# RWKV on one Trainium2 core: repeating a unit's values by DMA instead of by matmul, with the recurrence in place

## The chip, the core and the metric

The kernel runs on one core of one Trainium2 chip. A core has a matrix engine (PE, with a separate row in the profile, PEld, for its weight loads), a vector engine (DVE), an activation engine (ACT), a general engine (POOL) and a sequencer that only issues transfers (SP). Transfers that SP and ACT issue are carried by the same 16 DMA engines. The engines run on their own and meet at semaphores. The engines that compute read and write the on-chip memory SBUF, 128 partitions wide; matmuls write PSUM, which has 8 banks of 128 x 512 floats. DRAM is reached by DMA alone.

The metric is the time of one execution on the device in microseconds (us). All data is float32.

## What is computed

Four layers are applied in turn to x of shape 16 x 100 x 512 (batch, steps, channels): a cross attention, an RWKV block, a second cross attention with a feed-forward part, and a second RWKV block. The change touches the two RWKV blocks, which are alike. Of one block this part matters (h = 32 heads of s = 16 channels):

```python
r = (xr @ Wr.T).reshape(b, l, h, s_)
k = (xk @ Wk.T).reshape(b, l, h, s_)
v = (xv @ Wv.T).reshape(b, l, h, s_)
g = jax.nn.silu(xg @ Wg.T)
...
def step(s, rkvw):
    r_t, k_t, v_t, w_t = rkvw
    a = k_t[..., :, None] * v_t[..., None, :]
    out = jnp.einsum('bhi,bhij->bhj', r_t, u * a + s)
    s = a + w_t[..., :, None] * s
    return (s, out)
```

Each head so has a state of 16 x 16 numbers (i of k, j of v) for each of the 16 batch rows, and 100 steps that follow one another. Around it lie a layer norm, mixes of neighbouring steps, the projections with their 512 x 512 weights, a norm over each head, the output projection, and a channel block of three more 512 x 512 projections.

## The kernel before

The 16 batch rows are worked on in NG = 4 groups of G = 4, so that a row of T = 400 numbers holds 4 batch rows of L = 100 steps. The 512 channels are NC = 4 pieces of 128. A pair of group and piece is a chunk, C = 0 to 15. A chunk has 128 channels x 16 values of j, which are 16 rows of states for each channel; they are done in 8 units of 128 partitions x 2 rows x 400. There are 128 units a block, u = 0 to 127; `where(u)` (line 1129) gives a unit's chunk C, its j group jg (four of the sixteen j) and rp (which two of the four 32-channel rows, r, it takes). On a unit's 128 partitions lie 4 values of j times 32 channels (2 heads of 16).

A unit needs k, w and r of its channels, the same for all four jq of its partitions, and v of its four j, the same for all 16 i of a head.

- `projections` (line 799) computes k, w, v, r and the gate g of a group, and `store` (line 806) sends each 128 x 400 piece from ACT's queue into a DRAM tile `put[g]` laid out [chunk, r, 32 channels, T]. There are 20 such stores a group; those of group 0 come before the first unit, those of groups 1 to 3 beside the units of the group before.
- `enter(C)` (line 1089), four units before a chunk begins, loads v, k and r back as 128 x 400 pieces (`vc`, `kc`, `rc`) for the bonus term `u * a`, and `repeat(C, 0)`; `repeat(C, 1)` follows two units later. `repeat` (line 1099) fills `kr`, `wr` and `rr`, 128 x 2 x 400 each and three buffers each, by four transfers of 32 partitions for each operand: one for each jq. `gates` (line 1203) loads g back.
- `spread(u + 1)` (line 1132) repeats v on 16 partitions: two calls of `mm` (four matmuls in the trace) with a 0/1 matrix `sel` (line 691) put v of the four j into the two rows of a PSUM tile `vb`, shifted by one step; ACT then copies the initial state of each batch row into the first step.
- `product(u)` (line 1147): DVE multiplies `vb` by `kr` in PSUM. `scan(u)` (line 1156): two DVE scans, one a row, run the recurrence over `wr` and `vb` into an SBUF tile `a`; POOL multiplies `a` by `rr`.
- `gather` (line 1166), every second unit, sums over i by four calls of `mm` (eight matmuls in the trace) into the PSUM bank `acc`, and after a chunk `norm` makes the head norm and the gating on ACT, POOL and PE.

The loop at line 1231 writes the order of the work out by hand: `u` runs from -42 past 128, and between the parts of a unit `pieces`, a list of projections and channel-block work with costs in us, is taken until the budget `due` of the step is used up (2.5, 2.95 or 3.9 us). PE, DVE, ACT and POOL issue in that order, since `mm`, `vector`, `scalar` and `gpsimd` (lines 79 to 82) pin it. SP's instructions are not pinned: a scheduler puts its transfers where it finds them ready. PSUM holds two `vb` of two banks each, `acc`, and three banks `mm` for all else. When the time comes, `load(n, "Wfk", "Wfr", "Wfv")` (line 1248) fetches the three channel-block weights, 1 MB each, into a ring of five weight tiles.

Of the kernel before, what the change touches and what calls it, by code (L numbers as in the profile page):

```python
# [17 lines left out]
G = 4  # L18
# [17 lines left out]
def xattn_sequence(ctx: ExitStack, tc: tile.TileContext, d: dict, out: bass.AP):  # L36
# [42 lines left out]
    vector, scalar, gpsimd = InOrder(nc.vector), InOrder(nc.scalar), InOrder(nc.gpsimd)  # L79
# [556 lines left out]
    def rwkv(n, ws, next_weights, last):  # L636
# [6 lines left out]
        with ExitStack() as es:  # L643
# [6 lines left out]
            vbs = [psum.tile([128, 2, 512], F32, name=f"vb{i}") for i in range(2)]  # L650
            acc = psum.tile([128, 512], F32, name="acc")
            slots = Slots([psum.tile([128, 512], F32, name=f"mm{i}") for i in range(3)])
# [35 lines left out]

            fold = one.tile([128, 32], F32, name="fold")
            nc.vector.tensor_reduce(fold, ident.rearrange("p (r s) -> p s r", s=32), AX.X, ALU.add)  # L690
            sel = one.tile([128, 16, 32], F32, name="sel")
            for j in range(16):
                nc.vector.tensor_copy(
                    sel[:, j, :].rearrange("p (h i) -> p h i", i=16),
                    fold.rearrange("p (h j) -> p h j", j=16)[:, :, j : j + 1].to_broadcast([128, 2, 16]),
                )
# [101 lines left out]

            def projections(g, base):
                nm = f"{n}_{g}"  # L800
                to = put[g] = {
                    t: dram.tile([NC, 4, 32, T], F32, tag=t, name=f"d{t}_{nm}")
                    for t in ("k", "v", "r", "w", "g")
                }

                def store(t, c, tile):
                    nc.scalar.dma_start(out=to[t][c].rearrange("r p t -> (r p) t"), in_=tile)
# [163 lines left out]
            def channels(g, slot):  # L971
# [41 lines left out]
                def keys(co):  # L1013
                    def read(ps):
                        if co == 0:
                            st["kk"] = two.tile([128, NC, T], F32, tag="kk", bufs=1, name=f"kk_{nm}")
# [19 lines left out]
                def values(i):  # L1036
                    b = g * G + i

                    def read(ps):
                        def add():  # L1040
# [3 lines left out]
                            if last:  # L1044
                                nc.sync.dma_start(out=out[b], in_=xb[b])
# [43 lines left out]
            def enter(C):  # L1089
# [4 lines left out]
                for k, bufs in (("v", 2), ("k", 1), ("r", 1)):  # L1094
                    t[k] = two.tile([128, T], F32, tag=f"{k}c", bufs=bufs, name=f"{k}c_{n}_{C}")
                    nc.sync.dma_start(out=t[k], in_=put[g][k][c].rearrange("r p t -> (r p) t"))
                repeat(C, 0)

            def repeat(C, rp):
                g, c = C // NC, C % NC  # L1100
                rep = chunks[C]["rep"][rp] = {}
                for t in ("k", "w", "r"):
                    rep[t] = two.tile([128, 2, T], F32, tag=f"{t}rep", bufs=3, name=f"{t}r_{n}_{C}_{rp}")
                    for jq in range(4):
                        nc.sync.dma_start(
                            out=rep[t][32 * jq : 32 * jq + 32],
# [124 lines left out]
            while u < UNITS + 6 or pieces or slots.due:  # L1231
# [15 lines left out]
                if u == UNITS - 32 - 3:  # L1247
                    cm.update(load(n, "Wfk", "Wfr", "Wfv"))
# [448 lines left out]
```

## Time and profile before

| what | value |
| --- | --- |
| median of 3 runs | 3563.27 us (3559.06 to 3570.37) |
| the profiled execution: its own time | 3563.91 us |
| its span in the profile | 3561.8 us |
| busy in the span: PE, PEld | 3252.8 (91%), 1434.5 (40%) |
| busy in the span: DVE, ACT, POOL | 1768.5 (50%), 972.8 (27%), 1374.2 (39%) |
| transfers issued by SP, share of the 16 engines | 177.59 MB, 17.3% |
| transfers issued by ACT, share of the 16 engines | 32.78 MB, 2.6% |
| PE's matmuls vb<-vc,sel: count, busy | 1024, 260.8 us |
| recurrence of block 1: first product, last multiply by r starts | 859.5 us, 1506.4 us |
| recurrence of block 3: first product, last multiply by r starts | 2819.4 us, 3465.6 us |

Busy time is the sum of the time in which an engine had an instruction of the program at work; idle time in front of a group says what ended it. An arrow `a<-b,c` names the tile written and those read, with buffer numbers left out. PE's matmuls are pipelined, so that a busy PE is not a PE at its peak. The time of the execution is 2.1 us more than its span. A window of the profile is a stretch of time from the span's start; it gives the busy time of each engine inside it, the granted PE clock (1.0 is full), the busy share of the 16 DMA engines, and the rate in GB/s.

### The profile page before, as it was taken

How to read it: one execution, taken by the hardware profiler on the slowest of the kernel's cores; microseconds unless marked ns; L12 is line 12 of the kernel's file. 1: busy time of each engine (PE TensorE's matmuls, PEld its weight loads, DVE VectorE, ACT ScalarE, POOL GpSimd, SP SyncE). 2: the span in 40 equal slices, each digit the busy share in tenths (PEclk: the TensorE clock that was granted, in tenths of full speed). 3: DMA queues.
4: the chain of work that ended last, by engine and by line, in shares of the span. 5: the costliest groups of instructions: out<-in, count | busy, mean ns of one | idle time of the engine just before them, and what ended most of it. 6: DMA issues, size and time to landing. Idle time of an engine off the chain costs nothing. (4 is left out here: it accounts for less than half of the span.)

```text
span 3561.8 us, 45408 instructions
## 1 busy us (share of the span) xinstructions
PE 3252.8 (91%) x17411; PEld 1434.5 (40%) x17411; DVE 1768.5 (50%) x3570; ACT 972.8 (27%) x1699; POOL 1374.2 (39%) x1036
## 2 busy tenths in 40 slices
PE   6999998868999988989999999699998899998898
PEld 3444443334333333334455455344443433333333
DVE  4777777723767755523333333400001386775551
ACT  1323222322333333322222322201111233333332
POOL 1444444543666655412212112200002366665541
PEclk8999999978999989989999999899998899998998
DMA  5010101022434342011000010200011243434300
GB/s 167 21 30 21 30 21 33 1 65 82 134 101 136 116 130 77 14 52 35 19 19 19 27 31 21 74 0 0 0 47 49 83 138 101 136 116 119 86 27 16
DMA packets 151074, 213.26 MB, mean 60 GB/s; under 512 B 22942, under 2 KB 131294, under 8 KB 150858
## 3 DMA queue, kind: packets, MB, share of 16 engines
q1 hardware_dynamic: 127818, 177.59, 17.3%
q10 hardware_dynamic: 23040, 32.78, 2.6%
q8 instruction: 137, 2.24, 0.3%
q14 instruction: 79, 0.65, 0.1%
HBM read 174.25 MB, written 36.04 MB: 59 GB/s over the span
## 5 line engine op out<-in xcount | busy, mean ns | idle before, releaser
L77 POOL TENSOR_TENSOR a<-a,rr 128x800 f32<-128x800 f32 x256 | 480.5, 1878 | 342.1 <-DVE a L77 265.4
L77 DVE TENSOR_TENSOR_SCAN a<-wr,vb 128x400 f32<-128x400 f32 x512 | 475.7, 970 | 19.3 <-PE acc L82 9.7
L77 DVE TENSOR_TENSOR vb<-vb,kr 128x792 f32<-128x792 f32 x256 | 250.5, 979 | 197.1 <-ACT vb L77 195.5
L77 DVE CUSTOM_DVE_ANT_0 junk<-l_sc,mask 100x361 f32<-100x361 f32 x512 | 273.0, 533 | 89.9 <-PE l_sc L82 73.4
L82 PE MATMUL vb<-vc,sel 32*128 32x396 f32 x1024 | 260.8, 566 | 2.4 <-ACT th L77 1.3
L77 DVE TENSOR_TENSOR pt<-l_sc,maskT 121x400 f32<-121x400 f32 x384 | 193.5, 566 | 91.9 <-PE l_sc L82 91.0
L77 ACT ACTIVATE pt<-pt 121x1600 f32<-121x1600 f32 x96 | 147.6, 1538 | 284.2 <-DVE pt L77 282.6
L1425 DVE CUSTOM_DVE_ANT_0 junk<-l2a_sc,mask 100x361 f32<-100x361 f32 x256 | 136.9, 535 | 173.0 <-PE l2a_sc L82 155.8
L63 PE MATMUL p<-l_proj,h 128*100 128x512 f32 x512 | 220.4, 593 | 0.0
L77 POOL TENSOR_TENSOR xj<-tm,ext 128x400 f32<-128x400 f32 x160 | 152.5, 960 | 170.3 <-DVE tm L77 165.2
L77 DVE SCALAR_TENSOR_TENSOR tm<-mm,vec,sx 128x400 f32<-128x400 f32 x160 | 99.8, 631 | 229.3 <-PE mm L82 184.3
L1617 DVE TENSOR_TENSOR x<-p,x 100x512 f32<-100x512 f32 x16 | 11.1, 691 | 379.3 <-PE p L63 340.2
L1461 POOL TENSOR_TENSOR pa<-pt,pt 121x1600 f32<-121x1600 f32 x16 | 57.2, 3573 | 366.7 <-ACT pt L1456 366.7
L63 PE MATMUL h<-yTb,l_fc 128*128 128x400 f32 x512 | 175.4, 505 | 7.9 <-ACT yTb L229 7.9
L82 PE MATMUL v<-l_v_w,ct 128*121 128x512 f32 x384 | 179.9, 614 | 0.0
L82 PE MATMUL k<-ct,l_k_w 128*128 128x361 f32 x512 | 172.8, 481 | 7.7 <-DVE mv_l2a L207 7.7
L77 POOL TENSOR_TENSOR pa<-pt,pt 121x1600 f32<-121x1600 f32 x32 | 114.7, 3583 | 167.0 <-ACT pt L77 167.0
L82 PE MATMUL l_sc<-kz,qz 32*100 32x361 f32 x1024 | 116.0, 523 | 42.6 <-DVE pt L77 21.6
L77 ACT COPY vb<-s0r 128x8 f32<-128x8 f32 x256 | 43.1, 168 | 408.7 <-PE vb L82 318.6
L82 PEld LDWEIGHTS vb<-vc,sel 32*128 32x128 f32 x1024 | 85.3, 190 | 145.5 <-issue 105.3
L63 PEld LDWEIGHTS p<-l_proj,h 128*100 128x100 f32 x512 | 85.7, 167 | 133.2 <-issue 132.6
L63 PEld LDWEIGHTS h<-yTb,l_fc 128*128 128x128 f32 x512 | 98.4, 193 | 82.9 <-ACT yTb L229 9.8
(254 smaller groups left out, 5317.3 us busy)
## 6 DMA issues: line engine op xcount, KB each, us to landing
kr<-dk SPq DMA_DIRECT2D x256, 100.0 KB
wr<-dw SPq DMA_DIRECT2D x256, 100.0 KB
rr<-dr SPq DMA_DIRECT2D x256, 100.0 KB
ct<-in_ctxT SPq DMA_DIRECT2D x32, 722.0 KB
dk<-k ACTq DMA_DIRECT2D x32, 200.0 KB
kc<-dk SPq DMA_DIRECT2D x32, 200.0 KB
dw<-wd ACTq DMA_DIRECT2D x32, 200.0 KB
dv<-v ACTq DMA_DIRECT2D x32, 200.0 KB
```

Of the source, the lines that this page charges most:

```text
L63: nc.tensor.matmul(out=ps, lhsT=lhs(c), rhs=rhs(c), start=(c == 0), stop=(c == n - 1))
L77: return lambda *args, **kw: tc.keep_in_program_order(op(*args, **kw))
L82: pin(nc.tensor.matmul(**kw))
L1425: nc.vector.tensor_tensor_reduce(out=junk, in0=ss[r][:L, :S2], in1=t["mask"], scale=-1.0, scalar=FLT_MAX, op0=ALU.add, op1=ALU.min, accum_ ...
L1461: nc.gpsimd.tensor_tensor(t["pa"], t["pt"][0], pt, ALU.add)
L1617: nc.vector.tensor_tensor(x, ps[:L, :], x, ALU.add)
```

## The change

- `sel`, `vb` and `spread` are gone. `fetch(u + 2)` loads a unit's v straight into its tile `a` by one transfer from DRAM, whose source names each row of 2 x 400 numbers 16 times; `first(u + 1)` lets ACT write the initial states into `a`. `product` multiplies `a` by `kr` in place, and the two scans run in place in `a`, which has six buffers instead of four. Source and destination of all of this are in SBUF.
- `repeat` uses one transfer for each operand, whose source repeats its 32 rows 4 times from the outside; the operands are now asked for one by one, at steps 4 to 7 of the chunk before, and r of the second half at step 0 of its own chunk. For this k, w, r and g lie in DRAM as [chunk, 32 channels, r, T], and v as one row of numbers, [chunk, j, h, r, T], one number late, so that a row read at its start gives the step before. `rows_of` makes the matching patterns: v's stores and loads become four transfers of 32 partitions each.
- SP's transfers of the RWKV blocks are pinned to source order. The channel-block weights are fetched in four parts each, one a step, from three fixed steps on.
- The five PSUM banks of `vb` and the three `mm` become seven `mm`, and `kk` moves into the ring of `xm`.

```diff
--- before.py
+++ after.py
@@ -76,7 +76,7 @@
...
-    vector, scalar, gpsimd = InOrder(nc.vector), InOrder(nc.scalar), InOrder(nc.gpsimd)
+    vector, scalar, gpsimd, sync = map(InOrder, (nc.vector, nc.scalar, nc.gpsimd, nc.sync))
@@ -647,9 +647,8 @@
...
-            vbs = [psum.tile([128, 2, 512], F32, name=f"vb{i}") for i in range(2)]
             acc = psum.tile([128, 512], F32, name="acc")
-            slots = Slots([psum.tile([128, 512], F32, name=f"mm{i}") for i in range(3)])
+            slots = Slots([psum.tile([128, 512], F32, name=f"mm{i}") for i in range(7)])
@@ -686,15 +685,6 @@
...
-            fold = one.tile([128, 32], F32, name="fold")
-            nc.vector.tensor_reduce(fold, ident.rearrange("p (r s) -> p s r", s=32), AX.X, ALU.add)
-            sel = one.tile([128, 16, 32], F32, name="sel")
-            for j in range(16):
-                nc.vector.tensor_copy(
-                    sel[:, j, :].rearrange("p (h i) -> p h i", i=16),
-                    fold.rearrange("p (h j) -> p h j", j=16)[:, :, j : j + 1].to_broadcast([128, 2, 16]),
-                )
@@ -796,15 +786,28 @@
...
+            def rows_of(g, t, c):
+
+
+                if t == "v":
+                    n0 = 1 + c * 128 * T
+                    rows = put[g]["v"][n0 : n0 + 128 * T].rearrange("(j h r t) -> r h j t", h=2, r=4, t=T)
+                    return [(slice(32 * r, 32 * r + 32), rows[r]) for r in range(4)]
+                return [(slice(0, 128), put[g][t][c].rearrange("p r t -> r p t"))]
+
             def projections(g, base):
                 nm = f"{n}_{g}"
                 to = put[g] = {
-                    t: dram.tile([NC, 4, 32, T], F32, tag=t, name=f"d{t}_{nm}")
-                    for t in ("k", "v", "r", "w", "g")
+                    t: dram.tile([NC, 32, 4, T], F32, tag=t, name=f"d{t}_{nm}")
+                    for t in ("k", "r", "w", "g")
                 }
 
+                to["v"] = dram.tile([NC * 128 * T + 1], F32, tag="v", name=f"dv_{nm}")
+                sync.dma_start(out=to["v"][0:1].rearrange("(p t) -> p t", t=1), in_=eps[0:1, :])
+
                 def store(t, c, tile):
-                    nc.scalar.dma_start(out=to[t][c].rearrange("r p t -> (r p) t"), in_=tile)
+                    for ps, rows in rows_of(g, t, c):
+                        nc.scalar.dma_start(out=rows, in_=tile[ps])
@@ -1013,7 +1016,7 @@
...
-                            st["kk"] = two.tile([128, NC, T], F32, tag="kk", bufs=1, name=f"kk_{nm}")
+                            st["kk"] = two.tile([128, NC, T], F32, tag="xm", bufs=3, name=f"kk_{nm}")
@@ -1042,7 +1045,7 @@
...
-                                nc.sync.dma_start(out=out[b], in_=xb[b])
+                                sync.dma_start(out=out[b], in_=xb[b])
@@ -1093,19 +1096,19 @@
                 t = chunks[C] = {"rep": {}}
                 for k, bufs in (("v", 2), ("k", 1), ("r", 1)):
                     t[k] = two.tile([128, T], F32, tag=f"{k}c", bufs=bufs, name=f"{k}c_{n}_{C}")
-                    nc.sync.dma_start(out=t[k], in_=put[g][k][c].rearrange("r p t -> (r p) t"))
-                repeat(C, 0)
-
-            def repeat(C, rp):
+                    for ps, rows in rows_of(g, k, c):
+                        sync.dma_start(out=t[k][ps], in_=rows)
+                repeat(C, 0, "k")
+
+            def repeat(C, rp, names):
                 g, c = C // NC, C % NC
-                rep = chunks[C]["rep"][rp] = {}
-                for t in ("k", "w", "r"):
+                rep = chunks[C]["rep"].setdefault(rp, {})
+                for t in names:
                     rep[t] = two.tile([128, 2, T], F32, tag=f"{t}rep", bufs=3, name=f"{t}r_{n}_{C}_{rp}")
-                    for jq in range(4):
-                        nc.sync.dma_start(
-                            out=rep[t][32 * jq : 32 * jq + 32],
-                            in_=put[g][t][c, 2 * rp : 2 * rp + 2].rearrange("r p t -> p r t"),
-                        )
+                    k = put[g][t][c, :, 2 * rp : 2 * rp + 2, :]
+                    sync.dma_start(
+                        out=rep[t], in_=bass.AP(k.tensor, k.offset, [[0, 4], [4 * T, 32], [1, 2 * T]])
+                    )
 
             def bonus(C, part):
 
@@ -1129,24 +1132,27 @@
             def where(u):
                 return u // 8, u % 8 // 2, u % 2
 
-            def spread(u):
+            def fetch(u):
 
                 C, jg, rp = where(u)
-                p4 = vbs[u % 2][:, :, :T].rearrange("p r (b t) -> p r b t", t=L)
-                for i in range(2):
-                    rs = slice(64 * rp + 32 * i, 64 * rp + 32 * i + 32)
-                    mm(
-                        out=p4[:, i, :, 1:L], lhsT=sel[rs, 4 * jg : 4 * jg + 4, :].rearrange("p q m -> p (q m)"),
-                        rhs=steps(chunks[C]["v"][rs, :])[:, :, 0 : L - 1], start=True, stop=True,
-                    )
+                g, c = C // NC, C % NC
+                a = products[u] = two.tile([128, 2, T], F32, tag="a", bufs=6, name=f"a_{n}_{u}")
+                v = put[g]["v"]
+                n0 = v.offset + ((c * 16 + 4 * jg) * 8 + 2 * rp) * T
+                sync.dma_start(out=a, in_=bass.AP(v.tensor, n0, [[4 * T, 8], [0, 16], [1, 2 * T]]))
+
+            def first(u):
+
+                C, jg, rp = where(u)
                 g = C // NC
                 scalar.copy(
-                    p4[:, :, :, 0], s0r[:, 2 * rp : 2 * rp + 2, C % NC, jg, g * G : (g + 1) * G]
+                    products[u].rearrange("p r (b t) -> p r b t", t=L)[:, :, :, 0],
+                    s0r[:, 2 * rp : 2 * rp + 2, C % NC, jg, g * G : (g + 1) * G],
                 )
...
             def product(u):
                 C, jg, rp = where(u)
-                p4 = vbs[u % 2][:, :, :T].rearrange("p r (b t) -> p r b t", t=L)
+                p4 = products[u].rearrange("p r (b t) -> p r b t", t=L)
@@ -1156,11 +1162,9 @@
             def scan(u):
                 C, jg, rp = where(u)
                 rep = chunks[C]["rep"][rp]
-                a = products[u] = two.tile([128, 2, T], F32, tag="a", bufs=4, name=f"a_{n}_{u}")
+                a = products[u]
                 for i in range(2):
-                    vector.tensor_tensor_scan(
-                        a[:, i, :], rep["w"][:, i, :], vbs[u % 2][:, i, :T], 0.0, ALU.mult, ALU.add
-                    )
+                    vector.tensor_tensor_scan(a[:, i, :], rep["w"][:, i, :], a[:, i, :], 0.0, ALU.mult, ALU.add)
                 gpsimd.tensor_tensor(a, a, rep["r"], ALU.mult)
@@ -1205,7 +1209,7 @@
...
-                nc.sync.dma_start(out=chunks[C]["g"], in_=put[g]["g"][c].rearrange("r p t -> (r p) t"))
+                sync.dma_start(out=chunks[C]["g"], in_=rows_of(g, "g", c)[0][1])
@@ -1244,13 +1248,16 @@
...
-                if u == UNITS - 32 - 3:
-                    cm.update(load(n, "Wfk", "Wfr", "Wfv"))
+                for k, at_u in (("Wfk", UNITS - 46), ("Wfr", UNITS - 40), ("Wfv", UNITS - 35)):
+                    if 0 <= u - at_u < NC:
+                        load_part(cm, n, k, u - at_u)
                 if u >= UNITS and not nws and not any(p[3] == ("wo", NG - 1) for p in pieces):
                     nws.update(next_weights())
                 unit = 0 <= u < UNITS
+                if 0 <= u + 2 < UNITS:
+                    fetch(u + 2)
                 if 0 <= u + 1 < UNITS:
-                    spread(u + 1)
+                    first(u + 1)
                 if unit:
                     product(u)
@@ -1260,12 +1267,17 @@
                 if 0 <= C < NC * NG:
                     if at == 4:
                         enter(C)
+                    elif at == 5:
+                        repeat(C, 0, "w")
                     elif at == 6:
-                        repeat(C, 1)
+                        repeat(C, 0, "r")
                         bonus(C, 0)
                     elif at == 7:
+                        repeat(C, 1, "kw")
                         bonus(C, 1)
                 C = u // 8
+                if 0 <= C < NC * NG and at == 0:
+                    repeat(C, 1, "r")
@@ -1620,6 +1632,11 @@
...
+    def load_part(ws, layer, k, c):
+        if c == 0:
+            ws[k] = wring.tile([128, NC, 512], F32, tag="w", name=f"l{layer}_{k}")
+        sync.dma_start(out=ws[k][:, c, :], in_=d[f"L{layer}_{k}"][c * 128 : (c + 1) * 128, :])
```

## The prediction

> **What bounds the kernel now.** I read the table of windows first, for the two stretches that the change touches: from the first product to the last multiply by r of either recurrence (columns: window, length, then busy us and count for PE, PEld, DVE, ACT, POOL, then granted clock, DMA share, GB/s).
>
> ```profile
> 859.50:1507.40 647.90, 609.22 (x2227) 229.22 (x2228) 440.00 (x542) 213.48 (x438) 401.65 (x328) 0.92 0.34 98
> 2819.40:3467.40 648.00, 609.96 (x2229) 230.44 (x2229) 439.95 (x542) 213.87 (x438) 402.31 (x327) 0.92 0.35 99
> ```
>
> PE is busy 609 of 648 us; DVE has 68%, POOL 62%, and the DMA engines 34% as a mean of sixteen. So PE sets the pace: 648 / 128 = 5.06 us a unit, 40.5 us a chunk. The groups and the waits of the first window say what follows PE there:
>
> ```profile
> L82 PE MATMUL vb<-vc,sel 32*128 32x396 f32 x508 | 128.6, 564 | 1.7 <-DVE a L77 1.1 <-ACT th L77 0.6
> L77 DVE TENSOR_TENSOR vb<-vb,kr 128x792 f32<-128x792 f32 x128 | 125.2, 978 | 97.8 <-ACT vb L77 97.0
> L77 DVE TENSOR_TENSOR_SCAN a<-wr,vb 128x400 f32<-128x400 f32 x256 | 237.9, 971 | 9.7 <-PE acc L82 5.0 <-DMA vc<-dv 0.9
> L77 POOL TENSOR_TENSOR a<-a,rr 128x800 f32<-128x800 f32 x128 | 240.2, 1878 | 170.7 <-DVE a L77 134.3 <-DMA rr<-dr 9.4 <-PE vb L82 5.8
> ```
> ```profile
> ACT vb L77 <- PE vb L82: 157.1, 89, 9.2
> ```
>
> ACT waits 157 us for PE's `vb`, DVE 97 us for ACT's first step in it, POOL 134 us for DVE's scan: a line of followers behind PE's spreading. The chain that ended last holds only 5% of the span, so I don't use it. Outside the recurrences the change touches only the front of each block.
>
> **The change, part by part: PE.** 128.6 us of vb matmuls go from each recurrence, 257 us in all. Were nothing else late, that is the gain's upper end. It can't all come: with PE at 609 - 129 = 480 us, DVE with 440 and POOL with 402 are close behind.
>
> **The transfers.** Per chunk the change issues 6 repeats and 8 fetches, each writing 128 rows of 3200 bytes, beside 3 + 3 loads and stores of 128 rows of 1600 bytes for k, r, g, one more store for w, and four loads and four stores of 32 rows for v. How many of the sixteen engines carry one transfer is the question on which all hangs. The trace shows that it need not be sixteen. Three looks at the transfers, a k store of 128 rows alone on the queues, an output of 100 rows alone, and the rate when the engines are full:
>
> ```profile
> DMA packets 144, 0.20 MB, mean 95 GB/s; under 512 B 16, under 2 KB 144, under 8 KB 144
> ```
> ```profile
> DMA packets 110, 0.20 MB, mean 68 GB/s; under 512 B 10, under 2 KB 10, under 8 KB 110
> ```
> ```profile
> 2298.00:2300.00 2.00, 0.00 (x0) 0.00 (x0) 1.26 (x5) 0.00 (x0) 1.26 (x2) 0.50 1.07 400
> 32.00:34.00 2.00, 0.87 (x8) 0.27 (x8) 1.90 (x7) 0.00 (x0) 0.00 (x0) 0.99 1.03 378
> ```
>
> The first has 128 packets of data and 16 small ones, the second 100 and 10: I read the small ones as one completion for each engine used, so 100 rows ran on ten engines. No transfer of the trace shows what a source with a repeating outer dimension does. [...] which engines are taken no row shows. [...] a repeat ([0,4] outermost) has 4 engines, a fetch ([4T,8]) 8, the k, r, w, g stores and loads ([r, p, t], r = 4) 4, and v's (h = 2) 2. [...]
>
> Price of a row: 378 to 400 GB/s over 16 engines are 23.6 to 25 GB/s each, mean 24.4: 0.066 us for 1600 bytes, 0.131 us for 3200. Engine 0 then has, per chunk:
> - repeats: 6 x 32 rows x 0.131 = 25.2 us
> - fetches: 8 x 16 x 0.131 = 16.8 us
> - k, r, g back: 3 x 32 x 0.066 = 6.3 us; v: 4 x 16 x 0.066 = 4.2 us
> - together 52.5 us; with the stores of the next group (4 x 32 and 4 x 16 rows) 12.7 us more, 65.2 us, against 40.5 us for a chunk now.
>
> A block has 16 x 52.5 = 840 us, plus stores beside 12 of the chunks, 12 x 12.7 = 152, plus 3 MB of weights over all sixteen, 8 us: **1000 us** where the recurrence takes 648. The excess is 352 us a block. Spread over sixteen engines the same work is 6 + 8 transfers x 8 rows x 0.131 + 9 x 8 x 0.066 = 19.4 us a chunk and hidden. [...] the 100-row output shows the same kind of limit. Ends for the price: 25 GB/s, and the k store's own rate (27.5% share over a look of 2.15 us, for 144 packets, makes about 22 GB/s): 976 and 1109 us a block. Pure throughput is a floor: the fetch runs two units ahead and a repeat at most four, while steps 4 to 0 ask for 46 of the 52.5 us, so engine 0 may idle in steps 1 to 3. But `a` has six buffers, SP can run on until a gather frees one, and stores fill such holes; I take no idle time and leave up to 5%, 50 us a block, to the range.
>
> **Front of a block.** The first product needs enter(0), kr, wr, rr and fetch(0) through engine 0: 8.4 + 3 x 4.2 + 2.1 = 23 us, of which the four steps from enter to unit 0 hide some 13 (850 to 859 is now nearly free of transfers): +10 us a block. The 16 copies into `sel` (0.17 us each) go, beside PE's projections: nothing.
>
> **DVE and POOL.** Product and scans now read two SBUF operands instead of one and a PSUM tile. Their bare time I leave at 978 and 971 ns: DVE's `x<-th,x`, both in SBUF, takes 692 ns at 512 elements, and so does `x<-mm,x` from PSUM. But that same row shows something else (timeline of the tail of block 1):
>
> ```profile
> 1470.54 1.87 POOL L77 TENSOR_TENSOR a<-a,rr 128x800 f32<-128x800 f32 x1
> 1470.58 0.69 DVE L77 SCALAR_TENSOR_TENSOR th_1b<-th_1b,mm 100x512 f32<-100x512 f32 x1 [2.56 <-PE mm L82]
> 1471.30 1.67 DVE L77 SCALAR_TENSOR_TENSOR x<-th_1b,x 100x512 f32<-100x512 f32 x1
> ...
> 1472.38 1.29 POOL L77 TENSOR_TENSOR sx_1b<-ext_1b 128x400 f32<-128x400 f32 x1
> ```
>
> DVE's SBUF-only `x` takes 1.67 us instead of 0.69: it ends 0.56 after POOL's multiply. POOL's `sx` (0.85 elsewhere) then ends 0.70 after DVE's. The `th` with a PSUM operand, in the middle of POOL's work, is not slowed, and no scan of the trace is (953 to 989 ns). [...] By the bare rows DVE and POOL lie beside each other, 440 and 402 us; [...] DVE's 128 x (0.978 + 2 x 0.971) = 374 us and POOL's 402 add up to 776 us a block, 128 more than now. That is 48.5 us a chunk, under engine 0's 52 to 65, and so mostly hidden behind it; if that cover is gone it decides.
>
> **Order and waits.** ACT's `first` now waits for a fetch; behind it on ACT stand the evacuations of projections, and PE waits for those once its seven banks are full. In SP's order a late buffer or store holds back every fetch behind it; the old SP waited 232.6 us for `vb` products at no cost, since nothing urgent was behind. These waits follow engine 0's pace and I add nothing. More `mm` banks and `kk` in the ring: nothing, PE is no longer the bound. In the last group PE's 49 us a chunk stay under 52.
>
> **Sum.** The profiled execution took 3563.9 us, 3561.8 of span and 2.1 around it; the median, 3563.3, is the same. 2 x (352 + 10) = 724: **4288 us**, 20% slower.
>
> **Rivals.**
> - Sixteen engines after all (or other engines in turn for each transfer): transfers hidden, the shared port decides, 3564 + 2 x 128 = 3820 us, and up to 3900 with handovers at 10% of the 776 more in one block. For it: no view names an engine. Against: the ten completions. 13%.
> - Faster: transfers spread and the port rarely contended because POOL waits 134 us for DVE anyway and slots into its gaps. Then half of PE's 257 us comes back (DVE's 440 us and the latencies keep the rest): 3564 - 129 = 3435 us. It decides only if a chunk's transfers stay under 36 us on the fullest engine and DVE's mean product under about 1.3 us. Against it stand both rows above. 6%.
> - Worse than throughput: bursts leave engine 0 idle, [...] port and engine add up in part: 4288 + 2 x (109 + 100) = 4700 us. 7%.
> - Engine 0 as summed: 74%, its own range 4180 to 4600.
>
> Range 3850 to 4620: it leaves out the faster case, part of the port case and the worst. What the measurement tells from no change is 0.3%, 11 us: faster 0.06, same 0.02, slower 0.92.
>
> **What would show it.** Recurrences of about 1000 us with a DMA share that stays low (under 0.5) while `a` is what DVE and ACT wait for; PE's busy time there down to 480; DVE's product and scans, and POOL's multiply, with means above 978, 971 and 1878 ns. A DMA share above 0.5 in recurrences of some 780 us would put me with the port; product at 980 ns and a shorter recurrence would make me wrong.

## The result and the profile after

The change makes the kernel slower: **4384.17 us** (median of 4 runs, 4380.6 to 4388.63) beside 3564.16 us for the kernel before on the same chip, a ratio of 1.23 (95% interval 1.2277 to 1.2324). The prediction was 4288 us. The profiled execution took 4382.49 us, with a span of 4380.6 us.

The table of windows of the kernel after, from the first product to the last multiply by r of either recurrence (columns as in the prediction: window, length, busy us and count for PE, PEld, DVE, ACT, POOL, then granted clock, DMA share, GB/s):

```profile
877.90:1915.00 1037.10, 595.52 (x1731) 226.58 (x1732) 570.28 (x543) 215.34 (x447) 503.25 (x335) 0.72 0.33 113
3247.70:4284.50 1036.80, 587.50 (x1733) 221.44 (x1734) 570.31 (x543) 215.09 (x447) 502.70 (x335) 0.73 0.33 114
```

Each stretch grew from 648 to 1037 us. In these 1037 us no compute engine is busy for more than 58%, and the DMA engines together show 33%: nothing in this row looks full. The groups of the page say what the engines stood still for:

```profile
L77 POOL TENSOR_TENSOR a<-a,rr 128x800 f32<-128x800 f32 x256 | 542.5, 2124 | 586.6 <-DMA rr<-dr 284.2
L77 DVE TENSOR_TENSOR_SCAN a<-wr,a 128x400 f32<-128x400 f32 x512 | 665.2, 1339 | 171.5 <-DMA wr<-dw 104.2
L77 DVE TENSOR_TENSOR a<-a,kr 128x792 f32<-128x792 f32 x256 | 325.0, 1270 | 640.6 <-DMA a<-dv 403.2
L77 ACT COPY a<-s0r 128x8 f32<-128x8 f32 x256 | 51.1, 202 | 1311.7 <-DMA a<-dv 1115.2
```

The followers of the PE matmul have become followers of transfers: in front of the ACT copy into the first step stand 1312 us of idle time, 1115 of them ended by the fetch of `a`. Before the scan it is `wr`, before the multiply `rr`. The three operations themselves are longer too (product 978 to 1270 ns, scan 971 to 1339, multiply 1878 to 2124).

Measured from first to last product, the places where the time went are:

| stretch | before | after | difference |
| --- | --- | --- | --- |
| start to first product, block 1 | 859.5 | 877.9 | +18.4 |
| first to last product, block 1 | 640.1 | 1030.2 | +390.1 |
| last product of block 1 to first of block 3 | 1319.8 | 1339.6 | +19.8 |
| first to last product, block 3 | 639.5 | 1029.3 | +389.8 |

They add up to 818 of the 819 us between the spans.

Two transfers alone on the queues show how many engines carry each, if a small packet is read as one engine's completion: a fetch near the end of block 3, with the packets from 4193.5 to 4198.5, and a k store of block 1 that ACT issued at 782.49, with those from 783.4 to 787.2:

```profile
DMA packets 136, 0.41 MB, mean 82 GB/s; under 512 B 8, under 2 KB 8, under 8 KB 136
a<-dv SPq DMA_DIRECT2D x1, 400.0 KB
```
```profile
DMA packets 132, 0.20 MB, mean 54 GB/s; under 512 B 4, under 2 KB 132, under 8 KB 132
q10 hardware_dynamic: 132, 0.20, 19.6%
```

128 rows of 3200 bytes and eight small completions: eight engines. 128 rows of 1600 bytes and four: four engines, where a k store of the kernel before had sixteen; its packets take 3.2 us from first to last, before 0.7. The packets of one chunk of the last group, between two stretches without any, are (1714.4 to 1770.3):

```profile
DMA packets 2413, 6.57 MB, mean 118 GB/s; under 512 B 108, under 2 KB 620, under 8 KB 2412
```

Its eight fetches, six repeats, three loads of k, r and g and four of v make these 108 with 8, 4, 4 and 2 completions each. Over the whole run 6719 packets have 4 bytes, 8 of them the data of `dv<-eps`. Four completions for each repeat, eight for a fetch, four for k, r, w and g, two for each of v's, ten for 100 rows, one for `dv<-eps` and sixteen for the rest make 6710, where 6711 are left.

### The profile page after: what moved, and what is told of

It is laid out like the page before. It is cut to its first block, busy times and chain, and to the rows that moved or that the text cites. A ratio compares the mean times of both kernels' runs of the same rounds, so it can differ in the third digit from the quotient of the medians.

```text
span 4380.6 us, 43316 instructions
## 1 busy us (share of the span) xinstructions
PE 3204.2 (73%) x16387; PEld 1411.6 (32%) x16387; DVE 2026.4 (46%) x3536; ACT 964.4 (22%) x1699; POOL 1568.6 (36%) x1036
## 5 line engine op out<-in xcount | busy, mean ns | idle before, releaser
L77 POOL TENSOR_TENSOR a<-a,rr 128x800 f32<-128x800 f32 x256 | 542.5, 2124 | 586.6 <-DMA rr<-dr 284.2
L77 DVE TENSOR_TENSOR_SCAN a<-wr,a 128x400 f32<-128x400 f32 x512 | 665.2, 1339 | 171.5 <-DMA wr<-dw 104.2
L77 DVE TENSOR_TENSOR a<-a,kr 128x792 f32<-128x792 f32 x256 | 325.0, 1270 | 640.6 <-DMA a<-dv 403.2
L82 PE MATMUL mm<-rk,ones 128*128 128x400 f32 x64 | 53.6, 941 | 413.0 <-POOL rk L77 370.9
L77 ACT COPY a<-s0r 128x8 f32<-128x8 f32 x256 | 51.1, 202 | 1311.7 <-DMA a<-dv 1115.2
L77 POOL TENSOR_TENSOR xj<-tm,ext 128x400 f32<-128x400 f32 x160 | 212.6, 1337 | 216.3 <-DVE tm L77 216.3
L82 PE MATMUL acc<-rk,center 128*32 128x400 f32 x256 | 46.5, 817 | 300.6 <-ACT sq L77 300.6
L82 PE MATMUL acc<-a,gat 128*32 128x400 f32 x1024 | 159.8, 626 | 12.1 <-POOL a L77 12.1
L82 PEld LDWEIGHTS mm<-rk,ones 128*128 128x128 f32 x64 | 16.5, 314 | 433.5 <-POOL rk L77 386.9
```

Of the source, the lines that this page charges most:

```text
L77: return lambda *args, **kw: tc.keep_in_program_order(op(*args, **kw))
L82: pin(nc.tensor.matmul(**kw))
```

## The experiments

E is the theory of the prediction: the fullest DMA engine sets the pace of the recurrences. That one engine takes a share of every repeat, fetch, store and load was not shown when the prediction was made, and engine 0 is a name for it: no view names an engine. P is its rival: DVE, with two operands in SBUF, and POOL take turns. The port that P speaks of is the author's picture, which no run shows; what is measured is that instructions of the two get longer beside each other (DVE's scan in place 1576 ns in e3, 1170 in e4, which leaves POOL's multiply out; 971 before, from PSUM). S, which some expectations name, is a second rival: a loop of waits that is walked one after the other, for which it doesn't matter how many engines carry a transfer. Times without an interval are single runs beside 3565 to 3573 us for the kernel before; recurrences are from first to last product, block 1 / block 3 (before: 640 / 640).

| version | us | recurrences |
| --- | --- | --- |
| the change | 4384 | 1030 / 1029 |
| e1 the change, no multiply by r | 4352 | 1018 / 1013 |
| e2 repeats on 16 engines | 4125 | 929 / 924 |
| e3 all on 16 engines | 3790 | 741 / 748 |
| e4 the same, no multiply by r | 3662 | 676 / 678 |
| e5 as e3, product in PSUM | 3748 | 715 / 710 |
| e6 as e5, loads earlier | 3738 | 703 / 713 |
| e7 the change, product in PSUM | 4406 | 1048 / 1049 |
| e8 the change, loads earlier | 4302 | 998 / 994 |
| e9 before, SP's order alone | 3565 | 640 / 640 |
| e10 the change, no fetches | 3976 | 804 / 824 |
| e11 as e5, repeats once | 3599 | 640 / 637 |
| e12 as e5, half the units by PE | 3610 | 639 / 634 |

### Port or engine 0: e1 and e7

e1 takes out POOL's multiply:

```diff
-                gpsimd.tensor_tensor(a, a, rep["r"], ALU.mult)
```

> The changed kernel with POOL's multiply by r left out (the gather sums the states themselves, so r's transfers arrive but nobody reads them). All transfers stay. Theory E, the fullest DMA engine sets the pace: engine 0 still has 51 us of rows a chunk and 64 with stores, so the time stays within 1.5% of 4384 us (4320 to 4400). Theory P, DVE and POOL taking turns at a shared port sets it: of the 776 us a block 240 go, and the recurrences fall from 1037 us to well under 900, the time to 4100 us or less. Theory S, a serial loop of waits (fetch, product, scan, multiply, gather, free buffer): 1.9 us go from a loop that is walked once in six units, some 40 us a block, 4300 us.

Measured 4352.46 us: 270 us of POOL's work a block are gone and the kernel gains 0.7%. e7 leaves POOL alone and keeps the change's transfers, but the fetch fills an SBUF tile and the product writes to PSUM, so that the scans read only one operand from SBUF:

```diff
-                a = products[u] = two.tile([128, 2, T], F32, tag="a", bufs=6, ...)
+                a = fetched[u] = two.tile([128, 2, T], F32, tag="vt", bufs=2, ...)
...
-                    vector.tensor_tensor_scan(a[:, i, :], rep["w"][:, i, :], a[:, i, :], 0.0, ...)
+                    vector.tensor_tensor_scan(a[:, i, :], rep["w"][:, i, :], vbs[u % 2][:, i, :T], 0.0, ...)
```

> The changed kernel, its transfers untouched, with the product written to PSUM as in e5 (two buffers for a fetched v instead of six for both). Theory E (the fullest engine): the port is hidden behind it, so the scan's mean goes back to about 970 ns but the time doesn't: 4330 to 4480 us, the upper part if the shorter ring of buffers lets engine 0 idle more. Theory P: the time falls below 4200 us.

4406.26 us. The scan's mean is back at 969 ns and the time is no better. As pace of the changed kernel, P falls by both.

### The transfers on sixteen engines: e2 and e3

e2 splits only the repeats, so that their outermost dimension has 32 rows instead of four copies (before the change, at 889.5 to 891.9, four such transfers of 32 x 2 rows left 256 packets of data and 64 small ones, sixteen each):

```diff
-                    sync.dma_start(
-                        out=rep[t], in_=bass.AP(k.tensor, k.offset, [[0, 4], [4 * T, 32], [1, 2 * T]])
-                    )
+                    for jq in range(4):
+                        sync.dma_start(
+                            out=rep[t][32 * jq : 32 * jq + 32],
+                            in_=bass.AP(k.tensor, k.offset, [[4 * T, 32], [1, 2 * T]]),
+                        )
```

> The changed kernel with each repeat of k, w and r sent as four transfers of 32 rows instead of one whose source repeats 32 rows four times; the same bytes and the same rows, 18 more issues by SP a chunk. Theory E: engine 0 has 6 rows x 8 instead of 6 x 32 a chunk, 18 us less, 33 us a chunk and 46 with stores; now the shared port (48.5 us a chunk) is about as late, so recurrences of 780 to 870 us and 3850 to 4050 us in all. Theory P or S: the distribution over engines doesn't matter, the time stays at 4330 us or more.

4125.24 us: a gain of 259, but 75 us over the upper end of what was expected. The windows of e2 and, from its waits, what ACT stood still for:

```profile
851.20:1787.50 936.30, 567.31 (x1732) 218.53 (x1733) 573.94 (x543) 216.08 (x447) 511.92 (x335) 0.76 0.46 128
```
```profile
ACT a L77 <- DMA a<-dv: 471.9, 76, 18.6
```

The fetches are still late for 472 us of a block, though by the prediction's prices engine 0 has only some 700 us of rows left a block (52.5 - 25.2 + 6 x 8 x 0.131 = 33.6 us a chunk, times 16, plus 152 of stores and 8 of weights). So what is left in e2 isn't engine 0's throughput alone, as summed. Two things in its trace bear on it, and neither was tried alone: the rows take longer (3200 bytes have a mean of 188 ns in this window, beside 146 in the changed kernel, and only 67 us are without any packet), and the transfers have become many. The traces show the transfers of SP and ACT on the same eight semaphores (1212 before the change, 1110 after it); of the 619 that SP issues in this window (333 in the changed kernel), 256 (78) were issued within 0.3 us after the one before on their own semaphore had landed.

e3 orders the 128 partitions as head, i, j instead of j, head, i, and writes every transfer with 16 or 32 outermost rows (two transfers for a repeat or a fetch, four for a store or a load):

```diff
...
+                    for h in range(2):
+                        sync.dma_start(
+                            out=rep[t][64 * h : 64 * h + 64],
+                            in_=bass.AP(k.tensor, k.offset + 64 * h * T, [[4 * T, 16], [0, 4], [1, 2 * T]]),
+                        )
...
+                for h in range(2):
+                    sync.dma_start(
+                        out=a[64 * h : 64 * h + 64],
+                        in_=bass.AP(v.tensor, n0 + 64 * h * T, [[0, 16], [4 * T, 4], [1, 2 * T]]),
+                    )
...
```

> The changed kernel with every transfer of the recurrence in a form whose outermost dimension is 16 or 32: a unit's partitions are ordered head, i, j instead of j, head, i, so that a repeat and a fetch are two transfers of 64 partitions each, and stores and loads are four of 32 rows. Same bytes, same rows, same work of DVE, POOL, ACT and (but for a few set-up matmuls) PE. Theory E plus P: engine 0 has 19 us of rows a chunk, hidden, and the port decides: recurrences of 776 to 860 us, 3820 to 4000 us in all, DVE's product and scans and POOL's multiply with means well above 980, 970 and 1880 ns. If the port costs little, PE's saving shows: under 3564 us. Theory S: above 4200 us.

3789.93 us: 594 of the 820 us come back, with the same bytes and more transfers. S, which expected over 4200 us here, falls. Its first recurrence and, from the groups there, the three operations (busy us and mean ns after the first bar, idle time after the second):

```profile
872.40:1620.70 748.30, 549.08 (x1733) 212.14 (x1734) 617.74 (x542) 217.41 (x447) 540.03 (x335) 0.83 0.59 157
```
```profile
L77 DVE TENSOR_TENSOR_SCAN a<-wr,a 128x400 f32<-128x400 f32 x256 | 393.5, 1576 | 21.6 <-ACT a L77 18.0
L77 POOL TENSOR_TENSOR a<-a,rr 128x800 f32<-128x800 f32 x127 | 289.8, 2283 | 157.8 <-DVE a L77 40.1 <-PE mm L82 26.2 <-DMA rr<-dr 18.7
L77 DVE TENSOR_TENSOR a<-a,kr 128x792 f32<-128x792 f32 x128 | 151.8, 1186 | 17.3 <-DMA a<-dv 16.6 <-DMA kr<-dk 0.5
```

The idle time in front of the product is down to 17 us, from 323 in the changed kernel's first recurrence, and the scan is now 1576 ns instead of 971, the multiply 2283 instead of 1878: with the transfers out of the way this is what shows.

### What is left of the loss: e4, e5, e6 and e11

e4 is e3 without the multiply by r.

> The kernel of the run before with POOL's multiply by r left out as well. If the port is what holds that kernel (776 us a block, 240 of them this multiply), the recurrences fall below 640 us and the time to 3350 to 3560 us, below the kernel before the change. If something else holds it (SP's issues, a wait for transfers), the time moves by less than 3%.

3662.23 us, 128 less than e3, but 100 over the upper end of what was expected: ACT still waits 191 us a block for fetches in it. e5 is e3 with the product in PSUM (the edit of e7, with three buffers for the fetched tile, and one less for two other tiles), e6 is e5 with v, k and r asked for at step 2 of the chunk before instead of step 4:

```diff
-                repeat(C, 0, "k")
...
-                    if at == 4:
+                    if at == (2 if C % NC else 4):
                         enter(C)
+                    if at == 4:
+                        repeat(C, 0, "k")
```

> The kernel of e3 (every transfer on sixteen engines) with the product written to PSUM: v and k are read from SBUF, the two scans read w from SBUF and the product from PSUM, as before the change. Transfers, PE's work and the multiply by r are those of e3; two PSUM pairs come back, three banks are left for the rest, and a few rings are a buffer shorter to make room. Port theory: only the product (128 x 0.98 = 125 us a block) still has two SBUF operands; 125 + 402 = 527 us of port, under DVE's 440 + and PE's 480 to 550 only by a little, so the port no longer decides: recurrences of 600 to 690 us instead of 748, and the scan's mean back at 970 to 1000 ns from 1576. In all 3480 to 3680 us. If the port cost nothing in e3 and the waits of the loop alone hold it, the time stays within 2% of 3790 us.

> e5 with the loads of v, k and r of a chunk asked for two steps earlier (except for the first chunk of a group, whose stores end late). If the wait of PE for the bonus product (77 to 97 us a block in e3 and e4) and SP's burst at steps 4 to 7 are what is left, the recurrences lose 30 to 70 us more and the time goes to 3420 to 3560 us, below the kernel before the change; if these waits are only where the lateness of something else shows, e5's time within 1%.

e5: 3747.89 us, ratio 1.0516 (1.0499 to 1.0534); e6: 3737.61, ratio 1.0482 (1.0467 to 1.0498). The gains that were named first failed to come, and both times fall where the alternative had them (within 2% of e3, within 1% of e5): the scans' second SBUF operand costs e3 42 us, not 110 or more (with what the fewer PSUM banks and buffers of e5 cost taken off), and asking earlier brings another 10. e5's first recurrence, and the same three operations:

```profile
878.20:1599.80 721.60, 556.05 (x1718) 214.19 (x1718) 478.21 (x542) 209.09 (x437) 454.33 (x329) 0.82 0.61 163
```
```profile
L77 POOL TENSOR_TENSOR a<-a,rr 128x800 f32<-128x800 f32 x128 | 270.5, 2116 | 143.9 <-DVE a L77 77.9 <-DMA rr<-dr 36.7 <-PE mm L82 9.9
L77 DVE TENSOR_TENSOR_SCAN a<-wr,vb 128x400 f32<-128x400 f32 x256 | 237.6, 969 | 19.0 <-DMA wr<-dw 12.4 <-PE acc L82 1.9 <-DVE vb L77 0.5
L77 DVE TENSOR_TENSOR vb<-vt,kr 128x792 f32<-128x792 f32 x128 | 167.5, 1309 | 174.7 <-DMA vt<-dv 82.6 <-ACT vb L77 70.4 <-DMA rr<-dr 10.4
```

The scan is cured (969 ns), the product (still two SBUF operands) is not (1309 ns, 978 before), and in front of it 175 us are idle, half for the fetch and half for ACT. Late transfers or hand-overs? e11 takes 15 of 16 chunks' repeats out of e5:

```diff
                 for t in names:
+                    if C:
+                        rep[t] = chunks[0]["rep"][rp][t]
+                        continue
```

> The version with all transfers on 16 engines and the product in PSUM (3748 us), with k, w and r repeated for the first chunk only: the other 15 chunks compute with the first chunk's values, so 180 of 192 repeats of a block (two transfers each) are left out. If late transfers in SP's queue are what holds that version at some 720 us a block, 3480 to 3620 us. If the hand-overs between ACT, DVE, POOL and PE hold it, within 1% of 3748: 3710 to 3785 us.

3599.39 us, the recurrences at 640 / 637, 75 and 73 us shorter than in e5: what e5 lost in each of them went with the transfers of the repeats. The windows and waits of e11:

```profile
878.66:1520.00 641.34, 535.52 (x1699) 207.37 (x1699) 468.01 (x538) 209.00 (x437) 462.76 (x328) 0.85 0.45 126
```
```profile
ACT vb L77 <- DVE a L77: 108.7, 37, 11.3
POOL a L77 <- DVE a L77: 98.2, 73, 8.3
DVE vb L77 <- ACT vb L77: 81.9, 31, 12.8
DVE vb L77 <- DMA vt<-dv: 15.3, 7, 5.0
```

Only 15 us of DVE's waits are for a fetch. But with PE freed of 129 us of matmuls the recurrence is as long as before: DVE, ACT and POOL wait for one another in a ring, and the gain that the change was to bring doesn't appear even where its transfers are hidden.

### The change in two parts: e9 and e10

e9 is the kernel before with SP's transfers of the blocks in source order:

```diff
-    vector, scalar, gpsimd = InOrder(nc.vector), InOrder(nc.scalar), InOrder(nc.gpsimd)
+    vector, scalar, gpsimd, sync = map(InOrder, (nc.vector, nc.scalar, nc.gpsimd, nc.sync))
```

> The kernel before, with one edit: SP's transfers of the RWKV blocks in source order. The prediction put nothing down for the order. If that holds, within 0.3% of before: 3555 to 3576 us, with recurrences of 640 us from first to last product. The rival, that in source order a transfer whose buffer comes free late holds back the repeats behind it, expects over 1% more: 3600 us and up, with DVE or POOL waiting for the repeats.

3564.85 us, ratio 0.9999 (0.9991 to 1.0008). The order alone does nothing.

e10 is the change with PE's `spread` put back:

```diff
...
-                if 0 <= u + 2 < UNITS:
-                    fetch(u + 2)
                 if 0 <= u + 1 < UNITS:
-                    first(u + 1)
+                    spread(u + 1)
...
```

> All of the change but the fetches: PE spreads v into PSUM as before, and the product stays in PSUM; repeats by one transfer each, stores, loads, layouts and SP's order as in the change. Engine 0 loses the fetches' 16.8 us a chunk: 16 x 35.7 + 152 + 8 = 731 us a block, to 780 with the idle time the change showed. So E: 3740 to 3880 us, DVE and POOL waiting for the repeats, no wait for values. If the fetches (their latency, or the shared port that comes with them) were what costs, nearly all of the loss goes: 3564 to 3620 us.

3976.4 us, 96 over the upper end: the repeats, the stores and the loads on few engines make half of the loss (412 of 820) without any fetch. The windows of e10's recurrences, ACT's waits in the first of them, and ACT's timeline at the end of its second chunk (start, us, engine, then what it did; ACTq are the transfers that ACT issues, and in brackets stands the idle time before):

```profile
892.70:1698.50 805.80, 648.35 (x2208) 238.45 (x2208) 435.42 (x538) 211.12 (x437) 400.21 (x326) 0.84 0.23 82
3047.10:3873.30 826.20, 663.77 (x2208) 245.23 (x2208) 437.17 (x538) 211.37 (x437) 399.85 (x326) 0.82 0.22 80
```
```profile
ACT vb L77 <- DMA vc<-dv: 61.4, 5, 19.2
ACT vb L77 <- DMA dv<-v: 54.9, 7, 15.0
ACT vb L77 <- DMA rr<-dr: 28.6, 2, 14.4
```
```profile
975.20 0.49 ACT L77 COPY v<-mm 128x400 f32<-128x400 f32 x1 [0.51 <-PE mm L82]
982.77 12.03 ACTq L821 DMA_DIRECT2D dv<-v  x4
994.90 0.27 ACT L77 COPY vb<-s0r 128x8 f32<-128x8 f32 x2 [19.21 <-DMA vc<-dv]
```

ACT copied a piece of v out of PSUM by 975.7, could begin its four stores at 982.8 only, and was done with them at 994.8. Two copies into `vb` stood behind them for 19 us, and with them DVE, POOL and PE. The four were issued less than 0.1 us after a transfer on the same semaphore had landed: two stores of ACT, then two loads `vc<-dv` of SP. A count of the packets under way in the first recurrence gives four in 59% of the time, six or more in under 5%, and none for 104 us (126 in block 3; stretches of over 0.3 us). Repeats, stores and loads, each on four engines, hardly ever add up to eight: they share the same four. 806 - 104 = 702 us with a packet under way stand beside the 731 that the prediction's prices give.

Where e10's idle time lies is seen by groups of four chunks. The times from first product to first product of each group in block 1 (the last one to the last product), and the rows of engine 0 by the prediction's prices, with the stores beside groups 0 to 2 and the weights put to group 2, are in us:

| group | before | the change | engine 0's rows in it | e10 | engine 0's rows in it |
| --- | --- | --- | --- | --- | --- |
| 0 | 139 | 262 | 261 | 192 | 194 |
| 1 | 149 | 263 | 261 | 205 | 194 |
| 2 | 166 | 276 | 269 | 221 | 202 |
| 3 | 186 | 230 | 210 | 186 | 143 |

In group 3 nothing is stored, and e10 takes as long there as the kernel before. The windows of group 3, before and in e10:

```profile
1313.60:1499.70 186.10, 173.89 (x593) 63.34 (x593) 110.42 (x134) 64.65 (x127) 98.16 (x79) 0.93 0.19 51
1510.10:1696.50 186.40, 174.19 (x593) 63.41 (x593) 110.41 (x134) 64.64 (x127) 98.14 (x79) 0.92 0.15 55
```

PE has 174 us of work there, engine 0 only 143, so PE sets the pace again and engine 0 idles for 71 of the 104 us. The expectation had put all sixteen chunks down to engine 0: that makes 43 of the 73 us by which the recurrence of block 1 exceeds 731. The rest, some 30, is in groups 0 to 2, where 30 us pass without a packet. (In block 3 group 3 takes 204 us; why wasn't tried.)

### Idle time of engine 0: e8

e8 makes e6's edit in the changed kernel.

> The changed kernel with the loads of v, k and r of a chunk two steps earlier, except at a group's first chunk. In the changed kernel no packet at all is in flight for 48 us a block, the idle time of the fullest engine that the forecast left out. If it comes from the loop that ends in PE waiting for the bonus product (192 us a block in the waits), a good part of it goes: 4290 to 4350 us. If it comes from elsewhere: within 0.7% of 4384 us. Under theory S (the loop of waits decides, not the engine's rows) much more goes: below 4250 us.

4301.9 us, 82 less (S expected below 4250): the recurrences are 33 and 35 us shorter, the fronts 3 and 9. The time in a recurrence with no packet under way (stretches of over 0.3 us), 48 us in the changed kernel, falls to 30. So 18 of some 33 us a block are such idle time, and 15 aren't accounted for.

### Half by DMA, half by PE: e12

The attempt at a version that gains: the even units of e5 are fetched, the odd ones are spread by PE.

```diff
...
-                if 0 <= u + 2 < UNITS:
+                if 0 <= u + 2 < UNITS and u % 2 == 0:
                     fetch(u + 2)
...
```

> The same version with 16 engines and the product in PSUM, but the odd units' values are spread by PE as before and only the even units' are fetched. PE gets back 64 us of matmuls a block, and a chunk has 8 transfers fewer. If late transfers hold the version at 3748 us, this is faster than it: 3540 to 3680 us. If the hand-overs hold it, it stays at 3700 to 3790 us. Faster than before only if PE's saving of 64 us a block is not lost to waits: below 3555 us.

3609.93 us, ratio 1.0131 (1.0114 to 1.0148). The windows of its recurrences:

```profile
886.10:1527.00 640.90, 567.73 (x1955) 216.15 (x1955) 453.31 (x538) 211.02 (x437) 427.48 (x328) 0.90 0.52 143
2863.80:3500.50 636.70, 562.14 (x1955) 214.95 (x1955) 454.46 (x538) 210.72 (x437) 426.28 (x328) 0.90 0.52 145
```

PE is busy for 42 and 48 us a block less than before, and the recurrences are 1 and 5 us shorter than before. The fronts take that and more: the first product comes 27 us later in block 1 and 19 in block 3 (the new partition order makes other matmuls for the initial states; how much of this they are wasn't tried). No version that was tried beats the kernel before.

## The prediction, point by point

- **Engine 0 sets the pace: right.** e3 shows it best: the same bytes in more transfers, but on sixteen engines, give back 594 of 820 us. Group by group the sum for engine 0 comes out as well, but for 20 us in the last group (the table at e10). The four, eight, four and two engines of the prediction were shown by no view of before; they held, in the eight completions of a fetch, the four of a k store, the 108 of a chunk and the sum of all (6711 beside 6710). That these transfers have an engine in common was not shown either; by e10's packets, four under way in 59% of the time and six or more in under 5%, transfers on few engines do fall on the same ones. Which ones these are no run shows. The prices held: rows of 3200 and 1600 bytes took 126 and 67 ns in the median, beside 0.131 and 0.066 us (their means in the recurrences are longer, 146 and 72 ns). Of the changed kernel's 1037 us, 48 have no packet under way; the other 989, the most that engine 0 can have been at work, stand beside the 1000 of the sum.
- **Idle time of engine 0: the term that was mis-sized.** The step read "I take no idle time and leave up to 5%, 50 us a block, to the range". It is 48 us a block; the rows took 11 less than their sum, and the difference is the 37 by which the window missed (1037 for 1000). Most of it lies at the two ends of the recurrence. In block 1 a hole of 16 us begins 12 us after the first product, while SP waits 32.6 us for PE's first gather to free a buffer of `a`; 19 us lie in the last 30 us of the window, where few rows are left to move; 14 us are in all between. So the three reasons given for zero (six buffers, SP running on, stores that fill holes) nearly held in the middle and failed at the start, and nothing was put down for the end. e8 leaves 11 us at the start, none in the middle and 19 at the end.
- **Front of a block: right in sign, half in size, and for another reason.** +10 was put down for the first unit's loads; it was +18.4 and +19.8. The first product in fact starts at 877.88, without a wait, when DVE is done with the statistics before it. What was late is ACT, at its stores of r and g before that (timeline of ACT in the changed kernel; ACTq are the transfers that it issues):

```profile
832.27 0.49 ACT L77 COPY r<-mm 128x400 f32<-128x400 f32 x1 [3.99 <-PE mm L82]
846.47 0.53 ACTq L810 DMA_DIRECT2D dr<-r  x1
847.04 0.50 ACT L77 ACTIVATE th<-mm 128x400 f32<-128x400 f32 x1 [14.28 <-DMA kr<-dk]
860.04 0.53 ACTq L810 DMA_DIRECT2D dg<-g  x1
860.66 0.50 ACT L77 ACTIVATE th<-mm 128x400 f32<-128x400 f32 x1 [13.12 <-DMA rr<-dr]
```

  The copy of r ended at 832.8 and its store was issued at 846.5; `th` stood behind it, DVE's gate behind `th`, the statistics behind the gate. Both stores were issued less than 0.1 us after a repeat that SP had issued on the same semaphore landed, `kr` at 846.39 and `rr` at 859.96, and these are also what the profile names in front of `th`. Of ACT's 256 stores in the changed kernel 115 were issued within 0.3 us after a landing on their own semaphore; before the change it was none of 160. So ACT's stores wait for earlier transfers, SP's slow ones among them, that count on the same of eight semaphores. This is read from the trace; no run gave ACT semaphores of its own. The prediction named evacuations and PE as what stands behind ACT's waits, but not that the stores themselves wait. With 2 x 38 for the recurrences and 18 for the fronts the miss of 96 us is accounted for.
- **Port hidden behind engine 0: right** (e1, e7). As the next bound once the transfers are spread it was oversized. The sum of bare rows, 776 us a block, was the author's estimate, with DVE and POOL in turn for the whole of every instruction in it. It isn't a floor: e3's window is 748 us, so they can't have taken turns for all of that. Of the 101 and 108 us by which e3's recurrences exceed those of before, 27 and 37 go with the scans' second SBUF operand (e5), and the other 74 and 71 with the repeats: e11, without most of them, is as short as before. The rival "sixteen engines, the port decides" named 3820 to 3900; e3 took 3790, and by e5 and e11 more for its repeats than for the scans' second SBUF operand. What the product's second SBUF operand costs, which e5 still has, wasn't tried alone.
- **Order of SP: nothing, right** for the kernel before (e9). In the changed kernel it wasn't tried by itself. More `mm` banks (the four of `vb`, not five, went to them) and `kk` in the ring weren't tried either.
- **Waits follow engine 0's pace: only in part.** With fetches in the queue they do. In e10 ACT stands still at its stores, and in groups 0 to 2, where engine 0 sets the pace, 30 us (41 in block 3) pass without a packet.
- **What would show it.** Recurrences near 1000, DMA share 0.33, `a` as what DVE and ACT wait for, the three longer means: all there. "PE's busy time there down to 480" was wrong: 596 and 588. The 496 matmuls did go (x2227 to x1731), but those left became longer, with the granted clock at 0.72 instead of 0.92.
- **Rivals.** The faster one, half of PE's 257 us back, needed hidden transfers, and DVE and POOL that don't slow each other. e11 has the first, and of the second the scan (970 ns; product and multiply still take 1262 and 2208), and its recurrences are as long as before: even so the gain doesn't come in this order of work. What holds e11 at 640 us, the ring of DVE, ACT and POOL or the hand-written budget of work per step, stays open.

## What to carry to other kernels

Before moving a repetition to DMA, write each transfer's source and destination as patterns and read the size of the outermost dimension: with 4 or 8 there, as here (four and eight completions for 128 rows), the mean DMA share says 33% while only 48 of 1037 us are without a packet, and the sum must be made for the fullest engine alone. The four copies that lead a repeat here are nearly half of the sum, 25 of 52.5 us a chunk; put the copies inside and a multiple of 16 rows outside (with 16 and 32 there, e3 got 594 of 820 us back). Make the sum by stages, and set it beside the other engines' work in each: in e10 the last four chunks are PE's again. Count as well who issues stores: an engine that computes stands still with its whole program order while its store waits, here for an earlier transfer, often one of SP's, on the same of eight semaphores (115 of ACT's 256 stores).

## What was not expected of the hardware

- **The granted PE clock is lower where PE is less busy**, in nearly all versions: PE's busy share and clock of the first recurrence are 94% and 0.92 before, 89% and 0.90 in e12, 84% and 0.85 in e11, 80% and 0.84 in e10, 77% and 0.82 in e5, 61% and 0.76 in e2, 57% and 0.72 after the change (only e3, 73% and 0.83, is out of line). Each matmul gets longer with it (`acc<-a,gat` 567 ns before, 622 after). So PE's busy time doesn't fall by what is taken from it: 129 us of matmuls went, and only 14 to 22 us of busy time. What sets the clock wasn't tried.
- **A fetch is long even alone.** In the isolated fetch shown above, sixteen rows an engine are 2.0 us at their median of 126 ns and 2.5 us at their mean of 153; from the first packet's start to the last one's end it takes 2.8 us, and from issue to that end 4.15 us. Four units of the recurrence before lasted 20 us, so that a wait of 15 to 20 us, as ACT has it, is several transfers in a line and not one slow one.
- **Other work of POOL gets longer too**: its `xj` (128 x 400, reading a tile of DVE) has a mean of 960 ns in the first recurrence before the change, 1457 in that of the changed kernel, and 1070 in e5's, where the scans read one operand from PSUM.
